# Four layers of cross attention and FFN on one core: the 32-head layer's output product as seven products of block sums

## The chip, the cores and the metric

The kernel runs on one core of one Trainium2 chip. The core has a matrix engine (TensorE, PE in the profile, with weight loads shown apart as PEld), three engines for elementwise work (VectorE or DVE, ScalarE or ACT, GpSimd or POOL) and a sync engine (SyncE, SP) whose queue issues nearly all of this kernel's transfers between HBM and the on-chip buffer (SBUF). Products land in the accumulation banks of PE (PSUM). Each engine runs its own instructions in its own order, and semaphores order them between engines. The metric is the device time of one execution in microseconds.

## The reference

Sixteen batches of 64 tokens with 512 channels pass four layers. Each layer is a cross attention and a feed-forward part, each on a layer-normalised input and added to x:

```python
x = x + L0_xattn(layernorm(x), ctx)   # windowed attention along the channels
x = x + L0_ffn(layernorm(x))          # int8 fake-quantised SwiGLU
x = x + L1_xattn(layernorm(x), ctx)   # 32 heads of 128, 8 key/value heads, RMS norm of q and k
x = x + L1_ffn(layernorm(x))          # MXFP4 fake-quantised product
x = x + L2_xattn(layernorm(x), ctx)   # 32 heads of 16
x = x + L2_ffn(layernorm(x))          # 64 low-rank experts, 16 of them per token
x = x + L3_xattn(layernorm(x), ctx)   # 16 heads of 96
x = x + L3_ffn(layernorm(x))          # 3-bit weights
```

The change is in the attention of L1:

```python
kv = concat([context, latents], axis=1)      # 64 + 64 tokens per batch
q = rms_norm(latents @ Wq) ; k = rms_norm(kv @ Wk) ; v = kv @ Wv
out = softmax(q k^T / sqrt(128)) v           # 8 kv heads, each with 4 query heads
return out.reshape(b, 64, 4096) @ Wo         # Wo is 4096 x 512
```

## The kernel before

Tokens lie in 8 tiles of 128 (two batches each), x0 to x7. All of x stays in SBUF in fp32; `kvT` holds, for each tile, the transposed normalised x (two blocks of 64) between the transposed context of its two batches.

There are two lanes of work. The *side lane* (`side`) runs layer 0 for all tiles, and then the later layers for tiles 0 to 3. The *main lane* (`main`) runs the attention of L1 for all tiles (`normed_attention`, L776) and then the later layers for tiles 4 to 7. Both are generators that yield the cost of what they have just written. `merged` (L1893) writes the program: after each yield of main it lets the side lane write work worth that cost times a rate, one rate for each group of tiles. PE runs its instructions in the order so written; on the other engines and on SP's queue a scheduler places them.

`normed_attention` takes the tiles in four groups of two, numbered 0 to 3. Group i waits until the side lane has finished layer 0 for its tiles. Within a group it goes over the 8 key/value heads and, for each, over the two tiles: 64 units (8 i + h, t). `ticks` (L208) runs a software pipeline over them. At index n, each step works on the unit that lies its lag behind:

- lag 0, `queries`: asks for the weights of this head and the next (`qkv_weights`, 1.5 MB each, L800) and for the rows of Wo of two heads earlier (`out_weights`, L806); loads kT and v of the context from where they were saved (L876, L881); multiplies with Wq (L884). `keys_values` (L903) multiplies with Wk and Wv. Statistics of q and k go through DVE (L825, L826) and a power on GpSimd (r, L125).
- lag 1, `scale` (DVE, L927) and `turn` (transposes of q and k, L143).
- lag 2, `scores` (L720) with the maximum (L731), the exponentials on ACT (L736) and the division by the sum on GpSimd (p, L745).
- lag 3, `turn_weights`; lag 4, `values` (L761), whose result ACT copies to aT (L956): for each of 4 query heads a block of 128 channels by 128 tokens.
- lag 5, `project`: four products of 128x512 (L770), one for each query head, with a head's 512 rows of Wo, added to x by DVE (`add_to`, L159).

The rows of Wo of one head are a tile l1a_o of 1 MB, in a pool tag "o" with two buffers, which the key and value weights for the context (`pair_weights`, L817) share. Before the units, and in between, the context's keys and values are computed and saved to DRAM (`context_keys`, L836).

In the side lane, for each pair of tiles, the window attention computes scores (dots), turns them through DRAM (att_d) and loads them as att, 16 loads of 512 KB a pair (L458) into four buffers. DVE multiplies these with shifted values (pv, L483), GpSimd adds up (acc, L493), and PE multiplies with Wo of L0 (ps_o, L324). Then the int8 FFN: xs on GpSimd (L591), transposes, a clamp of qT on GpSimd (L606), the products ps_gu (L634) and ps_dn (L671).

Of the kernel before, what the change touches and what calls it, by code (L numbers as in the profile page):

```python
# [8 lines left out]
F32 = mybir.dt.float32  # L9
# [6 lines left out]
ALU = mybir.AluOpType  # L16
AX = mybir.AxisListType

P = 128
B, S, D = 16, 64, 512  # L20
NTOK = B * S
NT = NTOK // P
NC = D // P
# [25 lines left out]
W2 = D // 2  # L49
# [5 lines left out]
class Block:  # L55
# [35 lines left out]

    def context(self, c, b):
        return self.kvT[:, c, b // 2, 3 * (b % 2), :]


class Lane:
# [607 lines left out]
class Attention:  # L704


    G = 4
# [65 lines left out]
        self.ln.add_to(t, ps)  # L773


def normed_attention(ln, groups, rates, w_in, w_kv, norms):  # L776

# [2 lines left out]
    k, nc = ln.k, ln.nc  # L782
    HD, NKV = 128, 8
    with ExitStack() as es:
        wpool = ln.pool(es, "l1w")
        pool = ln.pool(es, "l1a")
        at = Attention(ln, pool, HD)
        G = at.G
# [5 lines left out]
        NQ, NKVW = NC * G * HD, NC * 2 * HD  # L794
        w_qkv, w_o, kept = {}, {}, {}

        def qkv_weights(n):
            if n < NKV * len(groups) and n not in w_qkv:
# [4 lines left out]
                    w[:, NQ:].rearrange("p (c n) -> p c n", c=NC),  # L803
                )

        def out_weights(n):  # L806
            if n >= 0 and n not in w_o:
                w = wpool.tile([P, G * D], F32, tag="o", name=f"l1a_o{n}")
                nc.sync.dma_start(w, w_in[n % NKV, :, NQ + NKVW :])
                w_o[n] = w.rearrange("p (g n) -> p g n", g=G)  # L810

        dram = es.enter_context(
            ln.tc.tile_pool(name="saved", bufs=1, space=bass.MemoryType.DRAM)
# [2 lines left out]

        def pair_weights(hp):  # L817
            if hp < NKV // 2 and hp not in w_pair:
                w = wpool.tile([P, NC * 4 * HD], F32, tag="o", name=f"l1a_kv{hp}")
                nc.sync.dma_start(w, w_kv[hp])  # L820
                w_pair[hp] = w.rearrange("p (c n) -> p c n", c=NC)

        def factors(r, sq):

# [4 lines left out]
        def context_keys(u):  # L829
            hp, t = u  # L830
            pair_weights(hp)
            pair_weights(hp + 1)
            ps = ln.bank([P, 2, 2, HD], "ps_ckv")
            for c in range(NC):
                for j in range(2):
                    nc.tensor.matmul(  # L836
                        ps[j * S : (j + 1) * S],
                        lhsT=k.context(c, 2 * t + 1 - j),
                        rhs=w_pair[hp][:, c, :],
                        start=c == 0,  # L840
                        stop=c == NC - 1,
                    )
            n = NT * hp + t
            both = pool.tile([P, 2, 2, HD], F32, tag=("p", "pT", "aT")[n % 3], name="ckv", bufs=2)
            nc.scalar.copy(both, ps)  # L845
            sq = pool.tile([P, G, HD], F32, tag="qT", name="csq")[:, 0:2, :]
            nc.scalar.activation(sq, both[:, 0, :, :], AF.Square)
            r = ln.small.tile([P, 5], F32, tag="r", name="r")[:, 0:2]
            factors(r, sq)
            kept[u] = both, r  # L850
# [101 lines left out]
        def values(u):  # L952
            d = kept[u]
            ps = at.values(d.pop("pT"), d.pop("v"))
            aT = pool.tile([P, G, 2, S], F32, tag="aT", name="aT")
            nc.scalar.copy(aT.rearrange("p g b s -> p b g s"), ps)  # L956
            d["aT"] = aT

        def project(u):
            n, t = u  # L960
            out_weights(n)
            aT = kept.pop(u)["aT"]
            at.project(t, [aT[:, g].rearrange("p b s -> p (b s)") for g in range(G)], w_o[n])

        pair_weights(0)
        yield Need(1, 1.08)
# [9 lines left out]
        def rest(n):  # L976
            for _ in range(n):
# [3 lines left out]
        yield from ticks(  # L981
            [(NKV * i + h, t) for i, ts in enumerate(groups) for h in range(NKV) for t in ts],
            [
                (2, scores, 0.9),
                (1, scale, 0.0),
                (5, project, 3.4),
                (0, queries, 3.4),
                (1, turn, 0.7),
                (0, keys_values, 1.7),
                (4, values, 0.9),  # L990
                (3, turn_weights, 0.4),
            ],
            lambda u: needs.pop(u, None),
        )


def mxfp4_ffn(ln, tiles, w_in, bias, kept_w):
# [377 lines left out]
class BlockWeights:  # L1375
# [18 lines left out]
    def add(self, n):  # L1394
        blocks = [self.parts[n][:, i * W2 : (i + 1) * W2] for i in (0, 1, 2, 4, 3, 4, 5, 6)]
        yield from sums_of_blocks(self.ln, blocks[:4], blocks[4:])
# [183 lines left out]
class Q3Linear:  # L1580
# [46 lines left out]
    def product(self, t):  # L1627
        ln, nc = self.ln, self.ln.nc
        xT = self.kept.pop(t)
        ps = ln.bank([P, D], "ps_o")  # L1630
        for c in range(NC):
            nc.tensor.matmul(
                ps, lhsT=xT[:, c, :], rhs=self.wT[c], start=c == 0, stop=c == NC - 1
            )
        ln.add_to(t, ps)
        nc.sync.dma_start(self.out[t * P : (t + 1) * P, :], ln.k.x[t])
# [298 lines left out]
def decoder_kernel(ctx: ExitStack, tc: tile.TileContext, i: dict, out: bass.AP):  # L1935
    nc = tc.nc
# [84 lines left out]
    def main():  # L2021
        yield Need(0, 1.0)
        yield from normed_attention(
            a, groups, [0.85, 0.78, 0.78, 0.74], i["l1a_w"], i["l1a_kv"], i["l1a_n"]
        )
        yield Need(len(groups) + 2, 1.05)
        a.pages(ctx)
        yield from mxfp4_ffn(a, halves[1], None, i["l1f_b"], kept_w)
        weights = BlockWeights(a, i["sums_w"], kept_s)
        yield from small_head_attention(a, halves[1], i["l2a_w"], weights)  # L2030
        yield from last_layers(a, halves[1], weights)
# [104 lines left out]
```

## Time and profile before

| | |
|---|---|
| runs | 1610.2, 1613.09, 1616.97 us; median 1613.09 |
| the profiled execution's own time | 1614.41 us |
| its span, first to last instruction | 1612.6 us |
| mean granted clock of PE | 0.99 |
| busy: PE, DVE, GpSimd, ACT | 96, 63, 40, 39% of the span |
| first Wo product of L1, last | 223.1, 1082.7 us |
| moved by DMA | 220.98 MB, 137 GB/s mean |

A line of a group reads: source line, engine, operation, output<-inputs, tile shapes, number of instructions; then busy time in us and mean ns of one; then the idle time of the engine just before them, and what ended most of it. A line of the timeline reads: start in us, duration in us, engine, line, operation, and the number of instructions merged into it (x8); what is in brackets is the idle time before and what ended it. A line with SPq is the issue of a transfer; the DMA rows of the page end with the size of one and the median time from issue to landing in us.

The first unit's query product starts at 174.3 us in the trace; units 8, 16, 32 and 48 start at 267.4, 373.5, 593.0 and 798.1 us. So a unit takes 11 to 16 us.

### The profile page before, as it was taken

The page shows a single profiled execution, that of the slowest core. Times are in us where ns is not written, and L with a number is a line of the kernel's source. Part 1 is how long each engine was busy: PE and PEld are TensorE (multiplying, and loading weights), DVE is VectorE, ACT ScalarE, POOL GpSimd, SP SyncE. Part 2 cuts the span into 40 slices and gives each one's busy share as a digit, 9 for nine tenths or more (in the row PEclk, how much of TensorE's full clock was granted, in tenths as well). Part 3 has the DMA queues.
Part 4 walks back from the last instruction along what each step waited for, and adds up shares of the span by engine and source line. Part 5 has one row for each costly group of instructions (what it writes and reads, how often), then busy time and mean ns, then how long its engine had stood idle before and what let it go on. Part 6 is the DMA issues. An engine that isn't in the chain of part 4 may idle for free.

```text
span 1612.6 us, 21994 instructions
## 1 busy us (share of the span) xinstructions
PE 1554.6 (96%) x7446; PEld 976.8 (61%) x7446; DVE 1016.5 (63%) x2133; ACT 624.5 (39%) x1951; POOL 637.9 (40%) x678
## 2 busy tenths in 40 slices
PE   7988999999999999999999999999999999999999
PEld 2323445665565655556566566577666688866886
DVE  7687478776777667787964365469344554732345
ACT  3323443434433444334444344421244433213441
POOL 2493226732276222763323642225232233331233
PEclk9999999999999999999999999999999999999999
DMA  8991449723595336964534852052211005221031
GB/s 240 284 267 66 138 133 252 231 75 134 171 279 147 115 125 167 275 188 142 187 105 157 273 187 76 31 186 104 76 37 42 29 4 173 60 98 46 24 116 41
DMA packets 107839, 220.98 MB, mean 137 GB/s; under 512 B 50000, under 2 KB 68304, under 8 KB 97104
## 3 DMA queue, kind: packets, MB, share of 16 engines
q1 hardware_dynamic: 107152, 218.80, 43.2%
q8 instruction: 60, 0.98, 0.3%
q10 hardware_dynamic: 576, 0.79, 0.2%
q14 instruction: 51, 0.42, 0.1%
HBM read 194.38 MB, written 25.17 MB: 136 GB/s over the span
## 4 chain that ended last, share of the span: by engine, by line
PE 68%; DVE 12%; DMA 8%; POOL 5%; ACT 3%; issue 3%; SPq 0%; ACTq 0%; POOLq 0%; DVEq 0%
PE ps_wo L770 9%; PE ps_q L884 9%; PE ps_q L1725 5%; PE ps_kv L903 5%; DMA att<-att_d 4%; PE ps_s L720 4%; PE ps_wo L1329 4%; PE ps_a L761 4%; PE ps_pT L143 3%; PE ps_v L1666 3%; PE ps_h L1329 3%; PE ps_k L1709 2%; PE ps_o L1329 2%; PE ps_wo L1241 2%; DMA sums_d<-sums 2%
## 5 line engine op out<-in xcount | busy, mean ns | idle before, releaser
L884 PE MATMUL ps_q<-l1a_w,kvT 128*128 128x512 f32 x512 | 233.9, 600 | 1.7 <-ACT kvT L178 1.7
L770 PE MATMUL ps_wo<-l1a_o,aT 128*128 128x512 f32 x512 | 232.5, 597 | 2.6 <-ACT aT L956 2.5
L736 ACT ACTIVATE p<-ps_s,mx 128x128 f32<-128x128 f32 x384 | 135.3, 368 | 211.3 <-DVE mx L731 202.6
L125 POOL TENSOR_TENSOR r<-r,mhalf 128x5 f32<-128x5 f32 (+1 forms) x96 | 102.3, 1065 | 246.7 <-DVE r L826 231.9
L745 POOL TENSOR_TENSOR p<-p,sm 128x512 f32<-128x512 f32 x96 | 102.6, 1069 | 209.7 <-DVE sm L744 193.0
L884 PEld LDWEIGHTS ps_q<-l1a_w,kvT 128*128 128x128 f32 x512 | 95.8, 192 | 119.8 <-issue 116.3
L770 PEld LDWEIGHTS ps_wo<-l1a_o,aT 128*128 128x128 f32 x512 | 93.1, 191 | 97.0 <-issue 93.8
L903 PE MATMUL ps_kv<-l1a_w,kvT 128*128 128x256 f32 x512 | 123.6, 385 | 3.6 <-DVE x L159 3.2
L493 POOL TENSOR_TENSOR acc<-acc,pv 128x512 f32<-128x512 f32 x96 | 120.9, 1285 | 9.3 <-DVE pv L483 8.4
L836 PE MATMUL ps_ckv<-l1a_kv,kvT 128*64 128x512 f32 x512 | 119.7, 610 | 4.2 <-ACT ckv L845 4.2
L825 DVE TENSOR_REDUCE r<-sq 128x5 f32<-128x640 f32 x64 | 52.4, 818 | 98.2 <-ACT sq L911 98.1
L903 PEld LDWEIGHTS ps_kv<-l1a_w,kvT 128*128 128x128 f32 x512 | 93.1, 192 | 17.7 <-DVE x L159 4.4
L892 ACT ACTIVATE sq<-ps_q 128x512 f32<-128x512 f32 x64 | 38.2, 597 | 167.8 <-PE ps_q L884 167.8
L125 POOL TENSOR_TENSOR rs<-rs,mhalf 128x1 f32<-128x1 f32 x64 | 37.1, 588 | 162.8 <-DVE rs L134 154.0
L483 DVE TENSOR_TENSOR pv<-att,ps_v 128x512 f32<-128x512 f32 x128 | 81.5, 677 | 24.0 <-DMA att<-att_d 22.1
L720 PE MATMUL ps_s<-kT,qT 128*128 128x128 f32 (+1 forms) x704 | 92.4, 276 | 0.6 <-ACT k_last L1714 0.5
L159 DVE TENSOR_TENSOR x<-x,ps_wo 128x512 f32<-128x512 f32 x76 | 51.4, 676 | 59.5 <-PE ps_wo L1241 41.0
L372 DVE TENSOR_TENSOR prod<-qs,kp 128x1024 f32<-128x1024 f32 x64 | 78.1, 1257 | 15.8 <-ACT qs L353 7.9
L1725 PE MATMUL ps_q<-kvT,l3a_w 128*128 128x256 f32 x384 | 87.4, 385 | 0.0
L720 PEld LDWEIGHTS ps_s<-kT,qT 128*128 128x128 f32 (+1 forms) x704 | 85.2, 192 | 3.4 <-issue 1.1
L752 DVE COPY pT<-ps_pT 128x512 f32<-128x512 f32 x96 | 64.3, 682 | 30.9 <-PE ps_pT L143 30.9
L1725 PEld LDWEIGHTS ps_q<-kvT,l3a_w 128*128 128x128 f32 x384 | 73.1, 193 | 11.2 <-issue 1.4
(232 smaller groups left out, 2989.7 us busy)
## 6 DMA issues: line engine op xcount, KB each, us to landing
l1a_w<-in_l1a_w SPq DMA_DIRECT2D x32, 1536.0 KB, 6.8
att<-att_d SPq DMA_DIRECT2D x64, 512.0 KB, 9.1
l1a_o<-in_l1a_w SPq DMA_DIRECT2D x32, 1024.0 KB, 5.3
w_sums<-sums_d SPq DMA_DIRECT2D x22, 512.0 KB, 6.2
w_sums<-in_sums_w SPq DMA_DIRECT2D x28, 384.0 KB, 3.9
s<-ckv SPq DMA_DIRECT2D x32, 256.0 KB, 4.3
l3a_w<-in_l3a_w SPq DMA_DIRECT2D x6, 1024.0 KB, 5.6
raw<-in_sums_w SPq DMA_DIRECT2D x11, 512.0 KB, 4.4
```

What stands on the lines that cost most here:

```text
L125: self.nc.gpsimd.tensor_tensor(out, v, self.k.mhalf[:, : v.shape[1]], ALU.pow)
L483: nc.vector.tensor_tensor(pv.rearrange("p (q w n) -> p q w n", w=2, n=L), att[:, a, :].rearrange("p (q w n) -> p q w n", w=2, n=L), spaced ...
L493: nc.gpsimd.tensor_tensor(sums, before, pv, ALU.add)
L720: nc.tensor.matmul(ps[:, i, :], lhsT=qT[:, i // 2, 2 * (i % 2) : 2 * (i % 2) + 2, :].rearrange("p g s -> p (g s)"), rhs=kTs[i // 2], start ...
L736: nc.scalar.activation(p[:, i, :], ps[:, i, :], AF.Exp, bias=mx[:, i : i + 1], scale=self.scale, accum_out=sm[:, i : i + 1],)
L745: nc.gpsimd.tensor_tensor(p, p, bc(sm, 2, P), ALU.mult)
L770: self.nc.tensor.matmul(ps, lhsT=a, rhs=wo[:, g, :], start=g == 0, stop=g == len(chunks) - 1)
L836: nc.tensor.matmul(ps[j * S : (j + 1) * S], lhsT=k.context(c, 2 * t + 1 - j), rhs=w_pair[hp][:, c, :], start=c == 0, stop=c == NC - 1,)
L884: nc.tensor.matmul(ps, lhsT=k.stream(c, t), rhs=w_qkv[n][0][:, c, :], start=c == 0, stop=c == NC - 1,)
L903: nc.tensor.matmul(ps, lhsT=k.stream(c, t), rhs=w_qkv[n][1][:, c, :], start=c == 0, stop=c == NC - 1,)
L1329: self.ln.nc.tensor.matmul(ps[:, i % 2], lhsT=a(e), rhs=w[:, b * W2 : (b + 1) * W2], start=e == 0, stop=e == len(self.rhs) - 1,)
L1725: nc.tensor.matmul(ps[:, j], lhsT=wq[:, c, (j0 + j) * P : (j0 + j + 1) * P], rhs=k.kvT[:, c, t : t + 2, 1:3, :], start=c == 0, stop=c == N ...
```

## The change

Take a pair of heads (n = 2m, 2m+1) and the two tiles of a group. The output product is then a 2x2 block product: a(i, j) is aT of tile i and head j, and b(j, k) is a head's rows of Wo for half k (256 columns) of the output. Before, these are eight block products, written as 16 products of 128x512 on PE. Now, in groups 1 to 3, they are seven block products of sums:

- sums of weights: t1 = b12 - b11, t3 = b22 - b12, t2 = b22 - t1, t4 = b21 - t3
- sums of activations: s3 = a11 - a21, s1 = a21 + a22, s2 = s1 - a11, s4 = a12 - s2
- products: a11 b11 and a12 b21 (one bank), s3 t3 and a22 t4, s2 t2 and s1 t1, and s4 b22.

Four of the products are gathered over the four head pairs of a group: two in unused ends of kvT, two in a tile acc. At the group's end eight additions on DVE bring them into x.

Group 0 keeps the direct product, in halves of 256 columns. During it GpSimd makes the differences of weights, 64 operations of 128x256 in regions of kvT that hold the context otherwise, and SP saves them to DRAM in 64 transfers of 128 KB. In groups 1 to 3 they are loaded from there, four blocks of 512 KB for each pair beside three blocks of Wo. The tag "o" now has four buffers of 512 KB. The overwritten context is reloaded, 16 transfers of 128 KB. The rates for the side lane change too.

```diff
+    def between(self, t, n=1):
+        first = (4 * t + 3) * S
+        v = self.kvT.rearrange("p c t f s -> p c (t f s)")
...
         def out_weights(n):
-            if n >= 0 and n not in w_o:
-                w = wpool.tile([P, G * D], F32, tag="o", name=f"l1a_o{n}")
-                nc.sync.dma_start(w, w_in[n % NKV, :, NQ + NKVW :])
-                w_o[n] = w.rearrange("p (g n) -> p g n", g=G)
+            if 0 <= n < NKV and n not in w_o:
+                w_o[n] = [out_block(n, j) for j in range(2)]
...
+        products = ("b11", "b21", "t3", "t4", "t2", "t1", "b22")
+        order = [(m, w) for m in range(NKV // 2, NKV // 2 * len(groups)) for w in products]
+        def load_blocks(n):
+            while order and len(blocks) < n:
+                m, w = order.pop(0)
+                h = 2 * (m % (NKV // 2))
+                if w[0] == "b":
+                    blocks[m, w] = out_block(h + int(w[1]) - 1, int(w[2]) - 1)
+                else:
+                    blocks[m, w] = block("l1a_t")
+                    nc.sync.dma_start(blocks[m, w].rearrange("p c n -> p (c n)"), saved_sums[h, w])
...
+        def sums_of_weights(c):
+            def step(u):
+                if not first_group(u):
+                    return
...
+                v, w = ("b12", "b11", "b22", "b12", "b22", 0, "b21", 2)[2 * i : 2 * i + 2]
...
+                nc.gpsimd.tensor_tensor(sums[m, i][c], chunk(v), chunk(w), ALU.subtract)
+            return step
+        def save_sums(u):
+            if first_group(u):
...
+                for c in range(NC):
+                    nc.sync.dma_start(
+                        d[:, c * W2 : (c + 1) * W2].rearrange("p (j n) -> p j n", j=2), sums[m, i][c]
+                    )
+        def lhs_first(u):
...
+                nc.gpsimd.tensor_tensor(s3, a11, a21, ALU.subtract)
...
+        def product(m, *pairs):
+            ps = ln.bank([P, 2, W2], "ps_wo")
+            for i, (a, w) in enumerate(pairs):
+                w = blocks[m, w]
+                for c in range(NC):
+                    nc.tensor.matmul(
+                        ps[:, i], lhsT=a[:, c], rhs=w[:, c], start=c == 0, stop=c == NC - 1
+                    )
+            load_blocks(len(blocks) + len(pairs))
+            return ps
+        def gather(m, out, ps):
+            if m % (NKV // 2) == 0:
+                nc.scalar.copy(out, ps)
+            else:
+                nc.vector.tensor_tensor(out, out, ps, ALU.add)
...
+        def project_first(u):
...
+            if i == 2:
+                a11, a12 = (kept[u[0] - 1 + j, t]["aT"] for j in range(2))
+                ps = product(m, (a11, "b11"), (a12, "b21"))
+                gather(m, ends[0], by_chunk(ps[:, 0]))
+                add(x[0][:, 0], ps[:, 1])
...
+            if i == 3:
+                s3, a22 = lhs.pop((m, "s3")), kept[u]["aT"]
+                ps = product(m, (s3, "t3"), (a22, "t4"))
...
+        def project_second(u):
...
+            if i == 2:
+                ps = product(m, (s2, "t2"), (s1, "t1"))
+                gather(m, acc, ps)
...
+            ps = product(m, (s4, "b22"))
+            add(x[0][:, 1], ps[:, 0])
...
+            return 1.7
...
             [
+                (4, turnover, 0.0),
                 (2, scores, 0.9),
+                (6, sums_of_weights(0), 0.0),
                 (1, scale, 0.0),
-                (5, project, 3.4),
+                (5, project_first, 3.4),
+                (7, project_second, 3.4),
+                (5, lhs_first, 0.0),
+                (6, lhs_third, 0.0),
+                (7, save_sums, 0.0),
+                (6, sums_of_weights(1), 0.0),
                 (0, queries, 3.4),
+                (6, sums_of_weights(2), 0.0),
                 (1, turn, 0.7),
+                (5, lhs_second, 0.0),
                 (0, keys_values, 1.7),
+                (6, sums_of_weights(3), 0.0),
                 (4, values, 0.9),
                 (3, turn_weights, 0.4),
             ],
             lambda u: needs.pop(u, None),
         )
+        reload(1)
...
-            a, groups, [0.85, 0.78, 0.78, 0.74], i["l1a_w"], i["l1a_kv"], i["l1a_n"]
+            a, groups, [0.85, 0.81, 0.81, 0.767], i["l1a_w"], i["l1a_kv"], i["l1a_n"], i["ctxT"]
```

## The prediction

> **What bounds the kernel now.** I read the page first (busy times, chain, groups), then the groups of GpSimd by shape, then three windows by engine, then the timeline round the Wo product and round the places where the new work is put, and last the DMA issues.
>
> ```profile
> PE 1554.6 (96%) x7446; PEld 976.8 (61%) x7446; DVE 1016.5 (63%) x2133; ACT 624.5 (39%) x1951; POOL 637.9 (40%) x678
> PE 68%; DVE 12%; DMA 8%; POOL 5%; ACT 3%; issue 3%; SPq 0%; ACTq 0%; POOLq 0%; DVEq 0%
> L770 PE MATMUL ps_wo<-l1a_o,aT 128*128 128x512 f32 x512 | 232.5, 597 | 2.6 <-ACT aT L956 2.5
> l1a_o<-in_l1a_w SPq DMA_DIRECT2D x32, 1024.0 KB, 5.3
> att<-att_d SPq DMA_DIRECT2D x64, 512.0 KB, 9.1
> ```
>
> PE is busy for 96% of the span and makes 68% of the chain that ended last. Line 770, the product changed here, is one of its two largest groups, and PE stood idle before it for only 2.6 us: the product is never late. The DMA rows matter because the change splits the first load and competes with the second.
>
> Three windows (stretch, us, then busy time of PE, weight loads, DVE, ACT and GpSimd, clock, DMA share, GB/s) lie in the output stages of layer 0, where the other lane loads att:
>
> ```profile
> 260.00:305.00 45.00, 45.00 (x180) 28.07 (x178) 33.69 (x61) 18.82 (x68) 36.70 (x31) 1.00 1.03 278
> 440.00:500.00 60.00, 58.99 (x234) 36.49 (x233) 46.26 (x78) 23.75 (x86) 44.99 (x39) 1.00 0.99 264
> 650.00:695.00 45.00, 43.18 (x171) 26.85 (x170) 36.26 (x56) 17.59 (x63) 35.51 (x30) 1.00 1.05 269
> ```
>
> GpSimd, at 40% over the span, is at 82, 75 and 79% here (36.70 of 45 us, and so on), and the DMA engines are at about 1. So PE is the bound, but in these stretches two other resources are near theirs. The clock is 1.00.
>
> The duration of a PE step is read from starts:
>
> ```profile
> 568.58 1.89 PE L903 MATMUL ps_kv<-l1a_w,kvT 128*128 128x256 f32 x8
> 570.31 0.60 PE L143 MATMUL ps_xT<-ident,xn 128*128 128x128 f32 x4
> ...
> 572.94 3.60 PE L770 MATMUL ps_wo<-l1a_o,aT 128*128 128x512 f32 x8
> 576.38 3.60 PE L884 MATMUL ps_q<-l1a_w,kvT 128*128 128x512 f32 x8
> ```
>
> Four products of 128x512 take 576.38 - 572.94 = 3.44 us, 0.86 each; four of 128x256 take 570.31 - 568.58 = 1.73 us, 0.4325 each. Half the width costs half, within 1%.
>
> GpSimd by shape (mean ns of one after the comma), and its timeline in the first group with the PE steps that wait on it:
>
> ```profile
> L493 POOL TENSOR_TENSOR acc<-acc,pv 128x512 f32<-128x512 f32 x96 | 120.9, 1285 | 9.3 <-DVE pv L483 8.4
> L1273 POOL TENSOR_TENSOR sums<-raw,sums 128x256 f32<-128x256 f32 x22 | 16.7, 761 | 0.9
> ```
>
> ```profile
> 181.79 1.33 POOL L125 TENSOR_TENSOR r<-r,mhalf 128x5 f32<-128x5 f32 x1 [4.77 <-DVE r L826]
> 185.62 0.60 PE L143 MATMUL ps_qT<-ident,qn 128*128 128x128 f32 x4
> 284.79 1.28 POOL L493 TENSOR_TENSOR acc<-pv 128x512 f32<-128x512 f32 x1
> 305.24 6.18 POOL L493 TENSOR_TENSOR acc<-acc,pv 128x512 f32<-128x512 f32 x5
> 312.88 1.95 PE L324 MATMUL ps_o<-acc,w 64*64 64x512 f32 x16
> 319.05 4.71 POOL L591 TENSOR_TENSOR xs<-xb,rv 128x512 f32<-128x512 bf16 x4
> 326.20 1.19 POOL L606 TENSOR_SCALAR qT<-qT 128x512 fp32r<-128x512 f32 x2
> 328.77 2.48 PE L634 MATMUL ps_gu<-w_l0f,qT 128*128 128x256 f32 x16
> 350.89 0.40 POOL L606 TENSOR_SCALAR qT<-qT 128x256 fp32r<-128x256 f32 x1 [6.67 <-ACT qT L605]
> 351.40 1.28 PE L671 MATMUL ps_dn<-w_l0f,qT 128*128 128x512 f32 x4
> ```
>
> Each of these PE steps starts within 0.1 to 2.5 us of the end of a GpSimd operation that it needs: this cover is thin.
>
> **1. The matmuls.** A head pair over two tiles is 4 products of four 128x512: 16 x 0.86 = 13.76 us. As seven products of four 128x256 it is 28 x 0.4325 = 12.11. Twelve pairs in groups 1 to 3: -1.65 x 12 = **-19.8 us**. Group 0 keeps the direct product in half widths: 16 times (8 x 0.4325 - 3.44) = +0.3. PE is 96 to 100% busy in the windows, so the saving counts wherever nothing else becomes late. The new rates of the lanes (0.81 for 0.78, 0.767 for 0.74) only keep the side lane's pace against a main lane whose steps weigh less; no term.
>
> **2. Differences of weights in group 0.** Four pairs x four differences x four chunks = 64 GpSimd operations of 128x256, at 0.743 us (between the 761 shown and 725, the mean without a sum tile among the operands): 48 us. GpSimd runs its instructions in order, so what counts is what each batch stands in front of. From the order of the built kernel:
> - Pair 0: t1 runs where GpSimd is idle. t3, t2 and t4 (12 operations, 8.9 us) stand ahead of the first unit's rsqrt (line 125). They need head 1's block, issued at 173.07 in the trace and landing 5.3 later, 178.4; done at 187.3; rsqrt 1.33, the scaling on DVE 0.69, small fills: 189.6 against 185.62, **+4**.
> - Pair 1: t1 ahead of a softmax scaling of unit 5 whose transposes follow units later: 0. The other 12 (8.9) stand among the acc additions of the second tile and ahead of unit 9's rsqrt; head 3's block, issued at 277.75 in a stretch where this load lands after 8.9, comes at 286.65, 1.9 after 284.79. Together 10.8; up to 4.7 of idle time can absorb, and ps_o at 312.88 has 1.5 of slack after the last addition (305.24 + 6.18): 4.6 to 9.3, **+6**.
> - Pair 2: t1 ahead of a rsqrt with idle time before it: 0. Then 12 operations (8.9) between the xs products and the two clamps at 326.20, which have 2.0 of room: **+7**. They are nearest to a plain insertion, so I take nearly all of it.
> - Pair 3: t1 stands ahead of the clamp at 350.89, and head 6's block can only be loaded when the Wo step of 342.23 to 345.7 frees its buffer; + 5.0 landing + 4 x 0.743 + 0.4 = 354.1 against 351.40: **+2.7**. The rest (12) stands ahead of a rsqrt of group 1: 373.5 + 5.3 + 8.9 + 1.2 = 388.9 against 384.4, with ps_qT not due before about 394: 0 to 4.5, **+1.5**.
>
> Sum +21. Bounds: +8 if later PE idle time (the page's slices of group 0 are at 8 to 9 tenths in places) takes up all that the single rows allow, +32 if nothing is absorbed.
>
> The trace shows one further price: DVE's line 826 takes 0.15 to 0.17 us by itself and 1.25 us at 689.51, beside a GpSimd addition of 2.50 us from 689.46; so operations of the two engines do block each other. The Trainium skill's page "SBUF — State Buffer", section "SBUF: two separate sides", says that the pair of ports which these engines share is held for a whole instruction. If each new GpSimd operation blocked DVE for its length, its rule would make it 64 x 0.74 + 48 x 1.28 = 109 us of DVE time, an estimate; DVE at 63% would mostly hide it.
>
> **3. Saves and reloads on SP's queue.** 64 saves of 128 KB, 8 more out-weight loads and 4 more pair loads in group 0; 84 block loads of 512 KB for 24 of 1 MB in groups 1 to 3, 16 reloads of context: 152 more issues. At 0.35 us (the out-weight issue at 173.07 took 0.34, the one at 277.75 0.53) that is 53 us of SP time, spread over 900. A waiting load holds up all behind it on SP: kT, v, qkv weights and att. Group 0's saves stand behind finished sums and before or after the att stage, not in it: 0. In groups 1 and 2 block loads stand between att loads, each waiting for a product that frees its buffer. The last att pair, issued at 483.30, would wait for the product of t2 and t1 at index 25, 490.2 - 2.3 = 487.9: 4.6 late; and seven 512 KB blocks per pair instead of two 1 MB are 1.75 times the bytes, in stretches with DMA at 0.99 and 1.05. Against it: ps_o at 506.06 has 3.0 of slack, of which PE's gain eats 2. **+4** for each of two stages, **+8** (0 if the slack holds; 16 if both the wait and the bytes count in full).
>
> **4. Sums of activations, gathering, the end.** 48 GpSimd additions of 128x512 at 1.28: three of four follow a product with PE work behind them. One stands ahead of xs in group 2: +1.3. A pair's four DVE additions of 128x512 (0.68 each) become one such and five of 128x256 (0.41): 2.7 us either way. Eight closing additions per group, 8 x 0.57 (the 128x256 in-SBUF row) = 4.6 us of DVE between the last product and the next reader (DVE is at 75 to 81% in the windows), hidden but for about 1 in each of three groups, and 1 for the last, which layer norm waits for. **+5** (0 to 12).
>
> **Sum.** -19.8 + 0.3 + 21.2 + 8 + 5 = +14.7. On the profiled execution's own 1614.41 us that is 1629.1. The median of the runs shown lies 1.3 below that execution (1613.09), so I predict **1628 us**, 0.9% slower. Own range of this case: 1619 (group 0's bound of 8) to 1640 (its bound of 32).
>
> **Rivals.**
> - *Other side: the insertions are hidden.* GpSimd has 60% of the span free, and a late step in group 0 can be made up if the side lane still has PE work ready. If term 2 is under 6 and term 3 nearly 0, PE's gain decides: 1613 - 19.8 + 5 = **1598 us**. For it: PE's line 770 never waits. Against: the rows of 312.88, 326.20 and 351.40, with 0.1 to 2.5 us of cover. It decides from a sum of terms 2 to 4 below 12.
> - *It cancels.* Half of the waits are absorbed: 11 + 4 + 4 against 19.5, **1613 us**, 1605 to 1621.
> - *SP becomes the bound.* Block loads wait for products and att loads for them, at three stages with kT and v loads behind; each stage loses its full 4.6 plus 3 x 512 KB at about 264 GB/s, 6 us: term 3 becomes some 25 to 30, **1648 us**. For it: DMA shares of 1. Against: the chain's largest groups name att but no kT or v load.
>
> **How the numbers follow.** Forecast 0.42, hidden 0.24, cancels 0.20, SP 0.14. Below 1598 lies half of the second (0.12), above 1645 some 0.08: the range is 1598 to 1645. A measurement of this kernel tells about 0.5%, 8 us, from no change. Faster by more: 0.25. Within: the cancelling case and the forecast's edge, 0.23. Slower: 0.52.
>
> **What would show it.** Right: line 770's successor has 128 half-width products in group 0 and 336 after, in steps of 0.43 us; from about 181 the first ps_qT late by 4 us; gaps of PE before ps_o, ps_gu and ps_dn of group 0 with releasers on GpSimd; unit 16 starting some 15 to 20 us later than 373.5; groups 1 to 3 each about 5 us shorter without, or equal with, their att waits. Wrong, if GpSimd's differences run in idle time and unit 16 starts before 380; or if the new products wait for blocks or sums (idle time before ps_wo well above 2.6 us); or if SP's waits grow by more than 30 us with kT or v late.

## The result and the profile after

The changed kernel takes 1651.68 us (median, 1650.21 to 1657.09; the kernel before beside it 1611.64), a ratio of 1.0254 with a 95% interval of 1.0213 to 1.0296. It is 40 us slower. 1628 was predicted, with a range that ended at 1645. One execution of the kernel before beside e1 to e4 (2301.94 us) and one of e15 (4084.84 us) were slow ones, which the ratios below leave out.

One correction to the description of the change: the code makes t4 = b21 - t2, not b21 - t3. No time depends on it.

From the page of the changed kernel, the busy times and the chain that ended last:

```profile
PE 1554.0 (94%) x7862; PEld 1067.4 (65%) x7862; DVE 1054.9 (64%) x2172; ACT 629.4 (38%) x1960; POOL 750.5 (46%) x790
...
PE 65%; DVE 14%; POOL 9%; DMA 6%; issue 4%; ACT 2%; SPq 1%; ACTq 0%; POOLq 0%; DVEq 0%
PE ps_q L903 7%; PE ps_wo L1082 6%; PE ps_q L1958 5%; PE ps_ckv L855 5%; PE ps_kv L922 5%; PE ps_s L729 4%; PE ps_a L770 4%; PE ps_wo L1562 4%; PE ps_pT L152 3%; PE ps_v L1899 3%; PE ps_k L1942 2%; PE ps_h L1562 2%; POOL kvT L1028 2%; DMA att<-att_d 2%; PE ps_wo L1113 2%
```

PE is busy for 1554.0 us, before 1554.6: the saving does not show in the sum, and the time without work on PE rose from 1612.6 - 1554.6 = 58.0 to 1649.3 - 1554.0 = 95.3. The difference of 37.3 is nearly the whole of the longer span (36.7). GpSimd went from 5 to 9% of the chain, and its new line 1028, the differences of weights, is named there.

One reason why PE's busy time did not fall is in the next view: span and mean granted clock, first of the kernel before, then of the changed one.

```profile
core 0: 1612.6 us, clock 0.990
```

```profile
core 0: 1649.3 us, clock 0.980
```

The products themselves became cheaper as predicted: PE's busy time on the lines of the product with Wo fell from 232.5 us (line 770 before) to 214.8 (60.9 on line 1113 in group 0, 153.9 on line 1082), -17.7. So all other work kept PE busy for 17.1 us more. The clock accounts for most of it. In the changed kernel's trace it stands at 0.50 in 14 stretches of 3.4 or 6.8 us, 64.8 us in all, and PE is busy for 55.8 of them; before, there are 8 such stretches, 30.7 us with 29.9 us of work. If work takes twice as long there, that makes (55.8 - 29.9) / 2 = 13 us, an estimate. The other 4 us are not explained.

Unit starts, from the query products in both traces, show where the time went:

| unit | before | after | later by |
|---|---|---|---|
| 0 | 174.3 | 171.6 | -2.7 |
| 2 | 190.6 | 193.5 | +2.9 |
| 11 | 301.4 | 313.0 | +11.6 |
| 13 | 331.1 | 350.3 | +19.2 |
| 16 (group 1) | 373.5 | 396.2 | +22.7 |
| 32 (group 2) | 593.0 | 607.5 | +14.5 |
| 44 | 750.2 | 778.6 | +28.4 |
| 48 (group 3) | 798.1 | 825.6 | +27.5 |
| 63 | 1027.3 | 1051.6 | +24.3 |
| end of span | 1612.6 | 1649.3 | +36.7 |

Group 0 lost 22.7 us by unit 16 (25.4 from unit 0). Of these 25.4 us, 15.1 are idle time of PE (23.8 for 8.7) and 10.3 longer busy time: five of the half-clock stretches, 23.9 us, lie here, and one of 3.4 us before. Group 1 gained 8.2, group 2 lost 13.0, the units of group 3 gained 3.2, and 12.4 were lost after unit 63.

**Group 0.** The timeline of GpSimd in the changed kernel; line 1028 makes the differences, 134 is the rsqrt r, 615 the clamp of qT:

```profile
178.15 5.88 POOL L1028 TENSOR_TENSOR kvT<-l1a_o,kvT 128x256 f32<-128x256 f32 x8
184.27 1.17 POOL L134 TENSOR_TENSOR r<-r,mhalf 128x5 f32<-128x5 f32 x1
291.37 2.77 POOL L1028 TENSOR_TENSOR kvT<-l1a_o 128x256 f32<-128x256 f32 x4 [2.59 <-DMA l1a_o<-in_l1a_w]
294.10 1.40 POOL L1028 TENSOR_TENSOR kvT<-l1a_o,kvT 128x256 f32<-128x256 f32 x2
296.68 1.41 POOL L1028 TENSOR_TENSOR kvT<-l1a_o,kvT 128x256 f32<-128x256 f32 x2
298.04 1.18 POOL L134 TENSOR_TENSOR r<-r,mhalf 128x5 f32<-128x5 f32 x1
339.78 5.19 POOL L1028 TENSOR_TENSOR kvT<-l1a_o,kvT 128x256 f32<-128x256 f32 x7
346.76 1.64 POOL L615 TENSOR_SCALAR qT<-qT 128x512 fp32r<-128x512 f32 x2
371.05 2.77 POOL L1028 TENSOR_TENSOR kvT<-l1a_o 128x256 f32<-128x256 f32 x4 [6.42 <-DMA l1a_o<-in_l1a_w]
373.78 0.40 POOL L615 TENSOR_SCALAR qT<-qT 128x256 fp32r<-128x256 f32 x1
```

PE in the same stretches:

```profile
186.32 1.09 PE L152 MATMUL ps_qT<-ident,qn 128*128 128x128 f32 x4 [3.24 <-DVE qn L946]
301.15 0.80 PE L152 MATMUL ps_qT<-ident,qn 128*128 128x128 f32 x4 [4.50 <-DVE qn L946]
347.87 2.46 PE L643 MATMUL ps_gu<-w_l0f,qT 128*128 128x256 f32 x15 [2.95 <-POOL qT L615]
```

Each time there is a batch of line 1028, then the rsqrt or the clamp, then PE's wait. Twice GpSimd itself waits first, 2.59 and 6.42 us, for a block of Wo to land, with everything behind it waiting too. PE's waits of 3.24, 4.50 and 2.95 us are shorter than the units' losses of 5.6, 8.6 and 7.6 in the same places. (Ahead of the third, PE also waits 3.21 us for the transposes of xs, at 337.74; before, 1.73.) What is missing is in the windows (stretch, length, busy time of PE, weight loads, DVE, ACT, GpSimd; then the clock, DMA share, GB/s), the changed kernel just after two of these waits:

```profile
187.00:190.00 3.00, 3.00 (x10) 2.46 (x10) 0.00 (x0) 0.86 (x2) 0.00 (x0) 0.50 0.07 20
302.00:306.00 4.00, 3.52 (x8) 2.70 (x9) 3.86 (x8) 0.94 (x2) 3.55 (x4) 0.50 0.40 116
```

After a wait PE is full, at half the clock.

**Group 2.** Lines 1052, 1059, 1066 and 1073 are the sums of activations, on GpSimd:

```profile
737.66 1.30 POOL L1052 TENSOR_TENSOR aT<-kvT 128x512 f32<-128x512 f32 x1
738.90 4.71 POOL L600 TENSOR_TENSOR xs<-xb,rv 128x512 f32<-128x512 bf16 x4
...
769.73 1.31 POOL L1059 TENSOR_TENSOR kvT<-kvT,aT 128x512 f32<-128x512 f32 x1 [7.70 <-ACT aT L977]
771.00 1.24 POOL L134 TENSOR_TENSOR r<-r,mhalf 128x5 f32<-128x5 f32 x1
772.20 1.26 POOL L1066 TENSOR_TENSOR kvT<-kvT 128x512 f32<-128x512 f32 x1
773.54 1.59 POOL L1073 TENSOR_TENSOR kvT<-kvT 128x512 f32<-128x512 f32 x1
776.10 1.04 POOL L754 TENSOR_TENSOR p<-p,sm 128x512 f32<-128x512 f32 x1 [0.96 <-DVE sm L753]
777.11 0.40 POOL L615 TENSOR_SCALAR qT<-qT 128x256 fp32r<-128x256 f32 x1
```

```profile
744.08 0.66 PE L152 MATMUL ps_q<-ident,xs 128*128 128x128 f32 x4 [2.56 <-DVE xs L607]
777.56 1.20 PE L680 MATMUL ps_dn<-w_l0f,qT 128*128 128x512 f32 x4 [3.62 <-POOL qT L615]
```

PE's row for the same product in the kernel before, without a wait:

```profile
745.56 1.18 PE L671 MATMUL ps_dn<-w_l0f,qT 128*128 128x512 f32 x4
```

One sum (1052) stands ahead of xs. Of the other three, 1059 stands ahead of the rsqrt r, and 1066 and 1073 ahead of the softmax scaling (754) and, behind it, of the clamp for ps_dn, before which PE waits 3.62 us. In between GpSimd is idle for 0.96 us: the scaling waits for DVE, where qn, which needs r, takes 1.73 us beside these sums (0.69 in the median of its 64). The prediction had the first sum and not the others.

At 688.2 PE waits 5.6 us for ps_qT. The chain there begins with an att load of 10.38 us and then runs through the closing additions of group 1:

```profile
670.47 10.38 DMA att<-att_d
...
684.77 1.45 DVE kvT L1103
...
686.25 3.11 DVE x L1103 x3
```

The same piece in the timeline:

```profile
679.56 7.77 POOL L502 TENSOR_TENSOR acc<-acc,pv 128x512 f32<-128x512 f32 x6
684.69 1.52 DVE L1103 TENSOR_TENSOR kvT<-kvT,acc 128x256 f32<-128x256 f32 x1
686.25 2.77 DVE L1103 TENSOR_TENSOR x<-x,kvT 128x256 f32<-128x256 f32 x2
```

An addition of 128x256 takes 1.52 us there beside GpSimd's additions; the same line with a product in PSUM as one input takes 0.41. So either the late att or the stretched additions could be behind the wait, which the runs below had to tell.

### The profile page after: what moved, and what is told of

The parts are those of the page before. It is cut to its first block, busy times and chain, and to the rows that moved or that the text cites. A ratio compares the mean times of both kernels' runs of the same rounds, so it can differ in the third digit from the quotient of the medians.

```text
span 1649.3 us, 23375 instructions
## 1 busy us (share of the span) xinstructions
PE 1554.0 (94%) x7862; PEld 1067.4 (65%) x7862; DVE 1054.9 (64%) x2172; ACT 629.4 (38%) x1960; POOL 750.5 (46%) x790
## 2 busy tenths in 40 slices
DMA packets 164038, 250.44 MB, mean 152 GB/s; under 512 B 60624, under 2 KB 121936, under 8 KB 157904
## 4 chain that ended last, share of the span: by engine, by line
PE 65%; DVE 14%; POOL 9%; DMA 6%; issue 4%; ACT 2%; SPq 1%; ACTq 0%; POOLq 0%; DVEq 0%
PE ps_q L903 7%; PE ps_wo L1082 6%; PE ps_q L1958 5%; PE ps_ckv L855 5%; PE ps_kv L922 5%; PE ps_s L729 4%; PE ps_a L770 4%; PE ps_wo L1562 4%; PE ps_pT L152 3%; PE ps_v L1899 3%; PE ps_k L1942 2%; PE ps_h L1562 2%; POOL kvT L1028 2%; DMA att<-att_d 2%; PE ps_wo L1113 2%
## 5 line engine op out<-in xcount | busy, mean ns | idle before, releaser
L745 ACT ACTIVATE p<-ps_s,mx 128x128 f32<-128x128 f32 x384 | 135.7, 370 | 232.5 <-DVE mx L740 213.5
L754 POOL TENSOR_TENSOR p<-p,sm 128x512 f32<-128x512 f32 x96 | 104.5, 1089 | 174.3 <-DVE sm L753 159.7
L922 PE MATMUL ps_kv<-l1a_w,kvT 128*128 128x256 f32 x512 | 129.7, 399 | 4.8 <-DVE acc L1092 1.9
L922 PEld LDWEIGHTS ps_kv<-l1a_w,kvT 128*128 128x128 f32 x512 | 97.3, 200 | 21.8 <-issue 5.1
L492 DVE TENSOR_TENSOR pv<-att,ps_v 128x512 f32<-128x512 f32 x128 | 82.1, 677 | 27.7 <-DMA att<-att_d 15.1
L381 DVE TENSOR_TENSOR prod<-qs,kp 128x1024 f32<-128x1024 f32 x64 | 82.0, 1321 | 15.6 <-ACT qs L362 8.1
L946 DVE TENSOR_TENSOR qn<-qn,r 128x512 f32<-128x512 f32 x64 | 60.9, 952 | 31.8 <-POOL r L134 31.6
L745 ACT ACTIVATION_READ_ACCUMULATOR p<-ps_s,mx 128x1 f32 x384 | 79.7, 208 | 0.0
L855 PEld LDWEIGHTS ps_ckv<-l1a_kv,kvT 128*64 128x64 f32 x512 | 33.9, 136 | 63.8 <-issue 60.5
```

What stands on the lines that cost most here:

```text
L492: nc.vector.tensor_tensor(pv.rearrange("p (q w n) -> p q w n", w=2, n=L), att[:, a, :].rearrange("p (q w n) -> p q w n", w=2, n=L), spaced ...
L745: nc.scalar.activation(p[:, i, :], ps[:, i, :], AF.Exp, bias=mx[:, i : i + 1], scale=self.scale, accum_out=sm[:, i : i + 1],)
L754: nc.gpsimd.tensor_tensor(p, p, bc(sm, 2, P), ALU.mult)
L855: nc.tensor.matmul(ps[j * S : (j + 1) * S], lhsT=k.context(c, 2 * t + 1 - j), rhs=w_pair[hp][c], start=c == 0, stop=c == NC - 1,)
L922: nc.tensor.matmul(ps, lhsT=k.stream(c, t), rhs=w_qkv[n][1][:, c, :], start=c == 0, stop=c == NC - 1,)
```

## The experiments

Each row's ratio compares with the kernel before on the same chip, whose median was 1611.59 to 1613.96 us beside e1 to e19; so differences between rows of different chips can be off by about 2 us. "Alone" stands for the seven products without the differences of weights, sums of activations and closing additions.

| kernel | us | ratio to before, 95% interval |
|---|---|---|
| changed | 1651.68 | 1.0254 (1.0213 to 1.0296) |
| e1 no differences | 1629.45 | 1.0090 (1.0064 to 1.0116) |
| e2 no sums of activations | 1640.35 | 1.0145 (1.0098 to 1.0192) |
| e3 no closing additions | 1653.79 | 1.0219 (1.0177 to 1.0262) |
| e4 alone | 1622.31 | 1.0047 (1.0018 to 1.0075) |
| e5 changed, rates 0.78 | 1644.28 | 1.0202 (1.0164 to 1.0240) |
| e6 changed, no block loads | 1641.69 | 1.0189 (1.0145 to 1.0232) |
| e8 alone, no block loads | 1605.27 | 0.9959 (0.9933 to 0.9984) |
| e9 before, rates of the changed | 1610.19 | 0.9998 (0.9978 to 1.0019) |
| e10 alone, small block loads | 1605.90 | 0.9946 (0.9931 to 0.9961) |
| e11 changed, sums of activations on DVE | 1641.31 | 1.0175 (1.0150 to 1.0200) |
| e12 changed, differences on DVE | 1637.23 | 1.0159 (1.0130 to 1.0189) |
| e14 alone, no loads, rates 0.78 | 1585.54 | 0.9824 (0.9808 to 0.9841) |
| e15 both on DVE, rates 0.78 | 1624.96 | 1.0060 (1.0036 to 1.0085) |
| e17 alone, loads, rates 0.78 | 1608.59 | 0.9968 (0.9947 to 0.9989) |
| e18 as e15, no block loads | 1607.22 | 0.9955 (0.9937 to 0.9972) |
| e19 as e15, differences split | 1624.82 | 1.0073 (1.0046 to 1.0100) |

### What the added elementwise work costs (e1 to e4)

Theory A: the loss comes from work on GpSimd and DVE that stands ahead of what PE waits for. Rival B: from the added transfers.

```diff
 # e1
-                nc.gpsimd.tensor_tensor(sums[m, i][c], chunk(v), chunk(w), ALU.subtract)
```

> The changed kernel without the 64 differences of weights on GpSimd; what is saved and loaded as t blocks is the context instead, so all transfers stay, and the output is not the reference's. Theory A (what is lost in group 0 is GpSimd's differences standing ahead of work that PE waits for): unit 16 starts at 373 to 377 us instead of 396.2, and the time falls by 18 to 24 us, to 1628 to 1634. Rival B (the saves, the split loads of Wo and SP's queue hold up group 0): unit 16 stays above 388 and the time above 1640.

Measured 1629.45, 22 us less; unit 16 starts at 372.1. Theory A, at the number. All transfers of group 0 are still there and cost nothing that shows: unit 16 is 1.3 us earlier than before the change, and group 0 takes 200.4 us, before 199.2. With the waits the half-clock stretches of group 0 are gone too, but for the one of 3.4 us that the kernel before also has.

```diff
 # e2
-                nc.gpsimd.tensor_tensor(s3, a11, a21, ALU.subtract)
...
-                nc.gpsimd.tensor_tensor(a21, a21, a22, ALU.add)
...
-                nc.gpsimd.tensor_tensor(a11, lhs[m, "s1"], a11, ALU.subtract)
...
-                nc.gpsimd.tensor_tensor(a12, a12, lhs.pop((m, "s2")), ALU.subtract)
+                lhs.pop((m, "s2"))
```

> The changed kernel without the 48 sums of activations on GpSimd; the products take the unsummed tiles, so the output is not the reference's. Theory A (sums stand ahead of xs and of the clamps of qT in group 2, where PE waited 2.6 and 3.6 us): these two waits go, group 2 takes 5 to 9 us less, the time is 1642 to 1647. Rival B (the waits of groups 1 to 3 come from transfers): no change beyond 3 us, 1649 to 1655.

Measured 1640.35, 11 us less by the medians, somewhat more than expected. The wait before ps_dn in group 2 falls to 1.3 us, that before xs also to 1.3.

```diff
 # e3
-                add(by_chunk(x[0][:, 0]), p1)
-                add(by_chunk(p6), p1)
...
-                add(p6, p5)
-                add(x[0][:, 1], p6)
```

> The changed kernel without the eight closing additions on DVE at the end of each group (the gathered products are never brought into x, so the output is not the reference's). Theory A (the additions of group 1, stretched to 1.5 us each beside GpSimd's acc additions, stand ahead of the statistics of q and make PE wait 5.6 us at 688, and again run at half clock after it): that wait falls below 1.5, the time is 1642 to 1647. Rival B (that wait is att landing late, 10.4 us after its issue): it stays at 4 us or more, and the time within 3 of 1652.

Measured 1653.79, no change, and PE's wait is still 5.4 us: theory A falls for this step. The additions are slow where they stand, and cost nothing that shows. That what is behind them waits for att anyway is the likely reason; e6 and e8 below bear on it.

> All three left out at once: the seven products, their gathering, all loads, saves and reloads stay. Theory A (the products themselves are as cheap as predicted, 18 to 20 us less PE time, and all that was lost came from the added elementwise work): 1590 to 1602 us, below the kernel before. Rival B (transfers hold up the groups too): 1608 to 1625.

The edits of e1, e2 and e3 together. Measured 1622.31, outside theory A's 1590 to 1602 and inside B's 1608 to 1625. With all elementwise work gone that A blames, the kernel is still 0.5% slower than before, although its products are cheaper. The wait at ps_qT in the att stage of group 2 is still there, with 5.4 us. So, against the predicted saving, something else costs nearly 30 us.

### Loads, and the pace of the side lane (e5 to e10, e14, e17)

```diff
 # e6, e8: after four blocks, no more loads
             while order and len(blocks) < n:
                 m, w = order.pop(0)
                 h = 2 * (m % (NKV // 2))
-                if w[0] == "b":
+                if len(fixed) == 4:
+                    blocks[m, w] = fixed[len(order) % 4]
+                elif w[0] == "b":
...
+                if len(fixed) < 4:
+                    fixed.append(blocks[m, w])
```

> The changed kernel, in which only the first four blocks of 512 KB are loaded and all later products read these again (80 loads fewer; the output is not the reference's). Theory B (loads of blocks on SP's queue between att loads, and their bytes, make att and the units' loads late in groups 1 and 2): the wait of 5.6 us at 688 falls below 2, and the time is 1638 to 1645. Rival (transfers are hidden, the rest is elementwise work): 1648 to 1655.

> The seven products alone (no differences, no sums of activations, no closing additions), and in addition only the first four blocks loaded; saves and reloads stay, the output is not the reference's. Theory B: 1600 to 1612, the wait of 5.3 us at 657 gone. Rival (what is left over the predicted 1593 comes from the elementwise work being squeezed together): 1617 to 1626, as with the loads.

Measured 1641.69 with everything else in place, 10 us less, though the intervals of the two ratios overlap a little; the wait at 688 shrank to 3.2 and not below 2, so theory B was right in the time and half right in the place. Alone, 1605.27: 17 us less than e4, well apart, and the wait is below 0.6. Alone, the block loads cost nearly as much as PE saves.

These are prices of all later block loads, not of the added ones. The kernel before loads Wo too, 24 MB in groups 1 to 3; the changed one loads 42 MB there, and the kernels without loads leave out 40. By their pages e8 moves 208.46 MB, the kernel before 220.98, the changed one 250.44. What the added 18 MB cost by themselves no run shows.

But how? In the changed kernel SP waits for the products before its block loads (line 999 loads t blocks, 821 blocks of Wo; us in total, times, longest):

```profile
SPq L999 <- PE ps_wo L1082: 88.7, 37, 10.5
...
SPq L821 <- PE ps_wo L1082: 70.4, 24, 22.6
```

That looks like a queue held up, the mechanism that the prediction priced. The next run keeps every load, in its place and with its wait, and takes the bytes away:

```diff
 # e10, on e4
+                if len(fixed) == 4:
+                    w_old = fixed[len(order) % 4]
+                    nc.sync.dma_start(w_old[:, 0, :64], w_in[h, :, NQ + NKVW : NQ + NKVW + 64])
+                    blocks[m, w] = w_old
...
```

> The seven products alone, with all 80 later block loads in their places on SP's queue and waiting for the same products, but with 32 KB each instead of 512 KB (the output is not the reference's). Theory B1 (the loads cost by standing on SP's queue, where they wait for a product while att, kT and v wait behind them): about as with full loads, 1618 to 1625. Theory B2 (they cost by their bytes, 40 MB beside att at a DMA share of 1): about as without loads, 1602 to 1609.

Measured 1605.90, as without loads, though SP still waits for the products ahead of the small loads (all of them are on line 999 here):

```profile
SPq L999 <- PE ps_wo L1086: 133.0, 57, 22.6
```

It is the bytes, not the queue: these waits on SP cost nothing that shows.

> The changed kernel with the side lane's rates of groups 1 and 2 back at 0.78 (0.767 stays). Theory C (the side lane's steps now come in less time, and its elementwise work, late, makes PE wait; a slower side lane gives it room): 1638 to 1646. Rival D (rates are neutral, the side lane's work is only shifted): 1647 to 1657.

```diff
 # e5, e14, e15, e17 to e19
-            a, groups, [0.85, 0.81, 0.81, 0.767], i["l1a_w"], i["l1a_kv"], i["l1a_n"], i["ctxT"]
+            a, groups, [0.85, 0.78, 0.78, 0.767], i["l1a_w"], i["l1a_kv"], i["l1a_n"], i["ctxT"]
```

> The kernel before with the rates of the changed one (0.85, 0.81, 0.81, 0.767), nothing else. Theory C (a faster side lane squeezes its elementwise work and PE waits): slower than before by 5 to 12 us. Rival D: within 4 us of before.

Measured 1644.28 for e5, in theory C's range, but the intervals of the ratios overlap those of the changed kernel, so this run alone settles nothing. e9 is the other way round, the kernel before with 0.81, 0.81 and 0.767: it does not mind them (0.9998), which is rival D. In the products alone the pace counts:

> The seven products alone, only the first four blocks loaded, and the side lane's rates of groups 1 and 2 at 0.78. If the predicted saving of 18 to 20 us on PE is to be had at all, this shows it: 1592 to 1600. If the gathering and the changed order of PE cost the rest whatever the rates: 1603 to 1610.

This is e8 with the rates of e5. Measured 1585.54, 20 us below e8 and 28 below before, more than the 18 to 20 expected. Its page and clock:

```profile
PE 1529.8 (97%) x7857; PEld 1053.8 (67%) x7862; DVE 1007.0 (64%) x2148; ACT 627.4 (40%) x1960; POOL 641.4 (40%) x678
```

```profile
core 0: 1583.7 us, clock 0.994
```

PE's busy time is 24.8 us below that of before: the saving of the products, and 6 us from a better clock (0.994 for 0.990). So the saving is to be had, where nothing is late. The 28 us flatter it, since this kernel moves 12.5 MB less than the kernel before.

> The seven products alone with all block loads and the rates of 0.78. Theory B2 (bytes cost by themselves, whatever the pace): 17 us over the kernel without loads at these rates, 1600 to 1606. Theory C (bytes cost only where the side lane's att stage comes too fast): 1586 to 1594.

This is e4 with the rates of e5, so e14 with all loads. Measured 1608.59, 23 us above e14 and a little above B2's range: the loads cost at the slower pace too (B2), and theory C, that they cost only because the side lane comes too fast, falls. The two traces show how. In the att stage of group 1, first without and then with the loads (windows, columns as above):

```profile
440.00:495.00 55.00, 55.00 (x253) 40.31 (x252) 44.05 (x76) 26.29 (x97) 44.31 (x38) 1.00 1.02 266
```

```profile
440.00:495.00 55.00, 49.27 (x215) 35.87 (x214) 37.76 (x66) 23.25 (x83) 37.33 (x32) 0.95 1.05 269
```

The DMA engines move 266 and 269 GB/s at shares of 1.02 and 1.05: the stretch was already full without the loads, and they push something else back. It is att. DVE's waits for it, without the loads and with them (us in total, times, longest; the kernel before, with its 24 loads of 1 MB, has 22.1, 15 and 4.2):

```profile
DVE pv L492 <- DMA att<-att_d: 16.0, 10, 3.1
```

```profile
DVE pv L492 <- DMA att<-att_d: 38.1, 16, 7.4
```

And the chain with the loads, round the longest:

```profile
472.37 14.88 DMA att<-att_d
...
487.35 0.69 DVE pv L492
488.03 0.60 DVE pT L761
488.63 0.61 DVE mx L739
489.24 0.02 issue
489.27 0.20 DVE mx L740
489.46 0.60 DVE qn L946
490.07 0.14 issue
490.20 1.08 PE ps_qT L152 x4
```

An att load lands 14.88 us after its issue (the median of all is 9.3 in this run). DVE stands at pv for 7.4 us, with the main lane's pT, mx and qn behind it, and PE, which needs qn for ps_qT, waits 5.7.

### The same work on the other engine (e11, e12, e15, e18, e19)

```diff
 # e11, and the same word in e12 at the differences
-                nc.gpsimd.tensor_tensor(s3, a11, a21, ALU.subtract)
+                nc.vector.tensor_tensor(s3, a11, a21, ALU.subtract)
```

> The changed kernel with the 48 sums of activations on DVE instead of GpSimd, 0.7 us each for 1.3. Theory A (they cost by what they stand ahead of on GpSimd: xs and the clamps of group 2): most of the 11 us that they cost comes back, 1640 to 1645. Rival (either engine is as full in these stretches, DVE at 76 to 81%, and it only moves the wait): 1648 to 1656.

Measured 1641.31, as without any sums (e2): on DVE they cost nothing that can be told.

> The changed kernel with the 64 differences of weights on DVE instead of GpSimd, about 0.57 us each for 0.74. Theory A (head of line on GpSimd, waiting for Wo's blocks): the wait moves to DVE, which has more behind it; the time comes out between 1645 and 1670, group 0 again 15 us or more longer than before. Rival (GpSimd is simply too slow for them): 1630 to 1638.

Measured 1637.23, outside A's range and at the edge of the rival's: of 22 us some 8 are left (e1 is the floor). Unit 16 starts at 379.2, against 372.1 without differences and 396.2 with them on GpSimd. So it mattered which engine had the work.

e15 has the edits of e11 and e12 and the rates of e5; e18 has the edit of e6 on top.

> The changed kernel, complete, with the side lane's rates of groups 1 and 2 at 0.78 and the sums of activations and differences of weights on DVE. If the single gains (7, 10 and 14 us) add up: 1617 to 1623. If they overlap, since each frees the same stretches: 1624 to 1635.

> The combined kernel (rates 0.78, sums and differences on DVE) with only the first four blocks loaded, so that the output is not the reference's. Theory B2: 10 to 17 us below the combined kernel. Theory C: within 5 of it.

> The combined kernel with the differences split, two chunks of four on GpSimd and two on DVE. If what they cost is the time that either engine is held in one piece in front of other work: 5 to 8 us below the combined kernel. If a wait on either engine is enough to make PE wait: the same or slower.

```diff
 # e19, on e15
-                nc.vector.tensor_tensor(sums[m, i][c], chunk(v), chunk(w), ALU.subtract)
+                (nc.vector if c % 2 else nc.gpsimd).tensor_tensor(sums[m, i][c], chunk(v), chunk(w), ALU.subtract)
```

Combined, 1624.96: the single gains of 7, 10 and 14 overlap by a few us. Splitting the differences changes nothing (1624.82). Without block loads 1607.22: again 18 us for the loads, as B2 has it, with all elementwise work in. The combined kernel is complete and 27 us faster than the changed one, but at 1.0060 (1.0036 to 1.0085) still slower than the kernel before. None of the complete versions beats that.

## Why the prediction was wrong

The sign, "slower", was right; the size, +15, was not (+40), and the time lies 7 us outside the range.

**The step that failed: every wait was priced at its own length.** The prediction read the clock in three windows, 1.00, and gave it no term. In the balance of PE the products give 17.7 us (19.5 predicted), idle time grows by 37.3 us (terms 2 to 4 had priced 34.2), and all other work takes 17.1 us more, some 13 of them in half-clock stretches: -17.7 + 37.3 + 17.1 = 36.7, the longer span. These last 17 us are most of what is missing between +15 and +40. That the idle time as a whole came out within 3 us is luck, since the terms 2 to 4 were off in different ways.

**Term 1, the products: right.** Two block products, eight of half width, take 3.46 us in the changed trace, 0.4325 each as predicted.

**Term 2, the differences: right in place, in size partly by luck.** +21 predicted, 22.7 by unit 16, and 22 by e1. By place: pair 0 +5.6 (predicted 4), pair 1 +8.6 (6), pair 2 +7.6 (7), pair 3 +3.4 and then +1.6 by unit 18 (2.7 and 1.5); unit 0 began 2.7 us earlier. But 21 was priced as waits alone, and of the 25.4 us of group 0 the idle time is 15.1; the rest is the slower clock after the waits.

**Term 3, the loads: wrong in mechanism, its size not settled.** The step that failed here is "The last att pair, issued at 483.30, would wait for the product of t2 and t1": waiting on SP's queue was given 4.6 us, and the bytes were named beside it and then priced only in the rival, at 6 us a stage. By e10 the waits cost nothing that shows. All later block loads together cost 10 us in the changed kernel, and 17 to 23 where less else is late; the +8 was for the added ones, which no run isolates. The rival "SP becomes the bound" came nearest in time, 1648, by luck: its 25 to 30 us for this term stand against at most 10 in e6. What it gave as its evidence, DMA shares of 1, was the right place to look.

**Term 4, sums, gathering and end: wrong item by item.** The 48 sums were priced at 1.3 us for the one that stands ahead of xs, "three of four follow a product with PE work behind them". They cost 11 (e2). What was overlooked is visible in the order: s1 stands ahead of the rsqrt, and s2 and s4 ahead of the scaling of p and the clamp for ps_dn, all within 5.4 us. The closing additions were given 4 us and cost nothing (e3). Beside GpSimd's additions of 1.3 us four of them take 1.37 to 1.52 us, and the two right behind 0.41. The Trainium skill's page "SBUF — State Buffer", section "SBUF: two separate sides", has a DVE operation with two inputs in SBUF and a GpSimd operation that reads SBUF lock each other out for whole instructions, and the trace agrees; but that time cost nothing. (The GpSimd addition of 2.50 us from 689.46 that the prediction names for this is two of 1.27 in the trace; its point stands.)

**The range.** The prediction's "own range" of 1619 to 1640 does not follow from its bounds of 8 and 32 for group 0, which give 1615 to 1639. The range that it stated does not rest on this.

**"No term" for the rates.** On the changed kernel the effect (7 us) is at the limit of what was measured; on the products alone it is 20 us without block loads (e8, e14) and 14 with them (e4, e17). Why the pace matters so much there and not in the kernel before (e9) was not settled. In the traces of e8 and e14, PE idles 68.4 and 54.0 us; the difference lies in groups 1 to 3 and behind them, where e8 has waits of 2.1 to 3.2 us at 800, 925, 1079 and 1109 that e14 has not.

**What stays open.** 12.4 us are lost after unit 63. PE is busy for 7.9 us more in that stretch, and idle for 4.5 more. Some 3.6 are only order: at the start of unit 63, 12 block products (20.8 us) remain to be done, and before the change five units (17.2). The idle time is in waits in the later layers, such as one of 3.55 us before a transpose at 1448; no run isolated their cause.

## What to carry to other kernels

A cheaper product is worth its PE time only where everything that feeds it is still early: in a kernel with PE at 96%, count the bytes that it adds to stretches where the DMA share is already 1, and look at which instruction of an in-order engine each new operation stands ahead of, one batch at a time. Price a wait of PE at more than its length if, as here, the clock often falls after it. And work that is put on the "free" engine by its mean busy share may be cheaper on the busier one, if that one's queue is early where it matters (10 us in e11, 14 in e12).

## What was not expected of the hardware

In the changed kernel 12 of the 15 waits of PE of 2 us and more (after its first instruction) were followed by 3.4 or 6.8 us at half the clock (0.50 in the windows at 187 and 302), in which one pass of 128x256 takes 0.63 us instead of 0.38; in the kernel before all 7 were. With those behind shorter waits, that adds up to 32 us of lost clock, and 16 before. The Trainium skill's page "TensorE: Matmul & The Clock Gate", section "Part 1: The HAM clock gate (the "warmup" mystery)", has the clock halved after an idle window of about 3.4 us and restored after a busy one of the same length. The lengths of the slow stretches agree; but here a wait of 2.46 us (at 251.4) was enough, and one of 3.62 us (at 773.9) had no slow stretch behind it. It is not the wait alone that decides: in e6 the same two waits, of 2.46 and 3.62 us, fell out the other way round.

Also, waits on SP's queue before block loads, 61 of them with 159 us in the changed kernel, look like the bottleneck and are none (e10 still has 57 with 133 us and the time without loads), while the bytes of these loads, 40 MB in under half of the span, cost 10 us in the changed kernel and 17 to 23 where less else was late.
